# Attention scores and greatest scores as single passes over exact high and low halves, with the shift as a pass of its own

## The chip, the cores and the metric

The kernel runs on one core of a Trainium2 chip. The metric is the device time of one execution in microseconds (us). Three runs of the kernel before gave 1910.36, 1911.48 and 1913.2 us; their median is 1911.48.

The engines of the core that matter here: TensorE (PE in the profile; its weight loads are PEld), VectorE (DVE), ScalarE (ACT), GpSimd (POOL), and Sync (SP), which here only issues DMAs. Each engine takes its instructions in order; they run beside one another and wait for one another by semaphores. TensorE writes its results to eight PSUM banks of 128 x 512 fp32.

## The reference

The model takes 2048 tokens of width 256 and a context of 1601 rows of width 192. A first layer lets the tokens attend to the context once and blends the result in with gates. A second layer, in which most of the time goes, is a transformer block:

```python
def _mha(q_in, kv_in, wq, bq, wk, bk, wv, bv, wo, bo):
    b = q_in.shape[0]
    q = (q_in @ wq.T + bq).reshape(b, -1, HEADS, HD).transpose(0, 2, 1, 3)
    k = (kv_in @ wk.T + bk).reshape(b, -1, HEADS, HD).transpose(0, 2, 1, 3)
    v = (kv_in @ wv.T + bv).reshape(b, -1, HEADS, HD).transpose(0, 2, 1, 3)
    scores = jnp.einsum('bhqd,bhkd->bhqk', q, k) * HD ** (-0.5)
    p = jax.nn.softmax(scores, axis=-1)
    o = jnp.einsum('bhqk,bhkd->bhqd', p, v)
    o = o.transpose(0, 2, 1, 3).reshape(b, -1, WIDTH)
    return o @ wo.T + bo
h = _layernorm(x, ln1_g, ln1_b)
x = x + _mha(h, h, sa_wq, ...)          # self-attention, 2048 keys
h = _layernorm(x, ln2_g, ln2_b)
x = x + _mha(h, context, ca_wq, ...)    # cross-attention, 1601 keys
h = _layernorm(x, ln3_g, ln3_b)
h = jax.nn.gelu(h @ mlp_w1.T + mlp_b1, approximate=False) @ mlp_w2.T + mlp_b2
return x + h
```

There are 16 heads of 16 features (HD). Everything is fp32. The softmax is a true one: each row's greatest score is subtracted.

## The kernel before

**Items and units.** The attention is cut into 32 *items*: one kind (`sa` or `ca`), one block of 512 queries, one group `g` of four heads. An item is cut into *units*, one for each 128 keys: 16 for self-attention, 13 for cross-attention (the last of these has 65 keys). `ITEMS` (L613) lists the items, `groups` (L625) all 464 units. Head `j` of a group has the 32 SBUF partitions from 32 x j on, 16 of which hold its features; so the four heads of a group use four different row groups of TensorE, and four matmuls run abreast.

**A unit.** `scores` (L718) computes keys x queries of one head into a bank, 128 keys by 512 queries, and ScalarE takes the exponential of it into a tile `pt` (L726). The row's greatest score must be subtracted before. It lies in a 17th row: the keys have rows of ones beside their features (`ones_beside`, L560) and the query tile `qa` has the negative greatest score in row 16 (`HD`) of each head, so the same matmul subtracts it. `values` (L731) multiplies the exponentials of the unit before with the values, four heads abreast in four column groups, into one bank, which ScalarE copies to `part` (L751) and GpSimd adds to the item's sum (L752).

**Greatest scores.** They are computed ahead, with the same products in the other orientation: `mx_block` (L664), 128 queries by 512 keys, reduced by VectorE straight from the bank (L680). `lead_unit` (L893) does such a group of four for the first `AHEAD` = 19 units before the attention loop starts; after that, each unit `u` of the loop does the four of unit `u + 19`, so the last 19 units have none. When an item's are complete, `mx_finish` (L701) reduces them, transposes them, sends them through DRAM and copies them into row 16 of `qa`.

**The order.** Compute instructions are kept in the order of the program by `kept`. `ORDER` (L629) is the order of one unit: score, greatest, score, greatest, and so on, then the values of the unit before. `later` (L633) hangs other steps onto the end of a unit: the divisions, the output projection, the layer normalisation of a finished block of queries, the next projection of queries (`q_block`, L639), and `q_spread`. Banks are given out in rotation (`bank`, L550), eight of them, nine to a unit. DMAs are not held to the program's order: they stand in their queue where the framework puts them, and start as soon as what they need is there and the queue has come to them.

**Queries and keys.** A projection gives eight heads on 128 partitions without gaps. `spread` (L592) copies the four heads of one group to their places by four DMAs of 16 partitions. `q_spread` (L657) does so for an item's queries, called four units ahead of the item's first greatest scores, into one of three tiles, plus a DMA that sets row 16 to zero. `k_sa_block` (L1063) does it for a block of 512 keys and half the heads, on the Sync queue, `k_ca_spread` (L1099) for the context's keys on ScalarE's queue.

**Ahead of the loop.** `FIRST` (L1117) is an order written out by hand of the gates of the first layer, the key and value blocks, the first queries and the leading units. The first layer itself, with `mean_context` (L363), comes before that. The MLP follows the attention.

Of the kernel before, what the change touches and what calls it, by code (L numbers as in the profile page):

```python
# [8 lines left out]
F32 = mybir.dt.float32  # L9
AF = mybir.ActivationFunctionType  # L10
# [4 lines left out]
P = 128  # L15
S = 2048
D = 256
# [12 lines left out]
EPS = 1e-5  # L30

# [39 lines left out]
def xattn_kernel(  # L71
# [464 lines left out]
    def load_wo(pool, w, name, queue):  # L536

        t = pool.tile([P, G // 2, D], F32, name=name)
        v = w.rearrange("(pr hf j w) n -> hf j w pr n", hf=2, j=4, w=HP)
        for hf in range(2):  # L540
            for j in range(4):
                r = j * HP + hf * HD
                dma = queue.dma_start(t[r : r + HD, :, :], v[hf, j, :HD])
                if queue is nc.gpsimd:
                    kept(dma)
        return t
# [13 lines left out]
    def ones_beside(queue, k, src, gs=range(G)):  # L560
        for g in gs:
            for j in range(4):
                queue.dma_start(k[j * HP + HD : (j + 1) * HP, g, :], src)

# [8 lines left out]
    nc.gpsimd.memset(hT_sa[:HD, 0, :], 1.0)  # L573
    ones_beside(nc.sync, k_sa, hT_sa[:HD, 0, :])
# [17 lines left out]
    def spread(queue, dst, src, hf):  # L592

        for j in range(4):
            r = (hf * 4 + j) * HD
            queue.dma_start(dst[j * HP : j * HP + HD], src[r : r + HD])
# [3 lines left out]
    shs, qa_bufs = [], []  # L600
    for i in range(2):
        sh = lead.tile([P, HP], F32, name=f"sh{i}")
        nc.gpsimd.memset(sh, 0.0)
        shs.append(sh)
    for i in range(3):
        qa = lead.tile([P, QB], F32, name=f"qa{i}")
        nc.gpsimd.memset(qa, 0.0)
        qa_bufs.append(qa)
    zero = lead.tile([4, QB], F32, name="zero")
    nc.gpsimd.memset(zero, 0.0)  # L610
# [18 lines left out]
    ORDER = "s0 m2 s1 m3 s2 m0 s3 m1 a".split()  # L629
    qas, mxps, oTs, hTs = {}, {}, {}, {"sa": {}, "ca": {}}  # L630
# [5 lines left out]
    def normed_block(pre, qb):  # L636
        return hT_sa[:, :, qb * QB : (qb + 1) * QB] if pre == "sa" else hTs["ca"][qb]

    def q_block(pre, qb):  # L639

        h = normed_block(pre, qb)
# [14 lines left out]

    def q_spread(n):  # L657
# [3 lines left out]
        spread(nc.sync, qas[n], normed_block(pre, qb)[:, g // 2, :], g % 2)  # L661
        nc.sync.dma_start(qas[n].rearrange("(j w) n -> w j n", w=HP)[HD], zero)

    def mx_block(n, i, j):  # L664
# [5 lines left out]
        mx = bank()  # L670
        if i < 4 * full:
            kb, qt = divmod(i, 4)
            mm(
                mx,
                qas[n][r, qt * P : (qt + 1) * P],
                kt[pre][r, g, kb * QB : (kb + 1) * QB],
                start=True,
                stop=True,
            )
            kept(nc.vector.tensor_reduce(mxps[n][:, j, qt, kb : kb + 1], mx, AX.X, ALU.max))  # L680
        else:
            left = L - full * QB
            for qt in range(4):
                mm(
                    mx[:, qt * left : (qt + 1) * left],
                    qas[n][r, qt * P : (qt + 1) * P],
                    kt[pre][r, g, full * QB :],
                    start=True,
                    stop=True,
                    skip_group_check=True,  # L690
                )
            kept(
                nc.vector.tensor_reduce(
                    mxps[n][:, j, :, full],
                    mx[:, : 4 * left].rearrange("p (t k) -> p t k", t=4),
                    AX.X,
                    ALU.max,
                )
            )

    def mx_finish(n):  # L701

        sh = shs[n % 2]
        kept(
            nc.vector.tensor_reduce(  # L705
                sh[:, :16].rearrange("p (j t) -> p j t", j=4), mxps[n], AX.X, ALU.max, negate=True
            )
        )
        shT = lead.tile([P, HP], F32, name="shT", bufs=2)
# [3 lines left out]
        nc.sync.dma_start(  # L713
            qas[n].rearrange("(j w) (t a x) -> w j t a x", w=HP, t=4, x=HP)[HD],
            d.rearrange("(a i j t) x -> i j t a x", a=4, i=2, j=4)[0],
        )

    def scores(u, j):  # L718
# [3 lines left out]
        r = slice(j * HP, (j + 1) * HP)  # L722
        sc = bank()
        mm(sc[:kw], kt[pre][r, g, k0 : k0 + kw], qas[n][r, :], start=True, stop=True)
        pt = work.tile([P, QB], F32, name="pt", bufs=8)
        kept(nc.scalar.activation(pt[:kw], sc[:kw], AF.Exp, scale=HD**-0.5))  # L726
        pts[u, j] = pt
# [98 lines left out]
    def norm_steps(kind, qb, ln, bias):  # L826
# [27 lines left out]
        def turn(c):  # L854

            if c == 0 and kind == "mlp":
                hTs.setdefault(kind, {})[qb] = hT_sa[:, :, qb * QB : (qb + 1) * QB]
            elif c == 0:
                hTs.setdefault(kind, {})[qb] = work.tile([P, 2, QB], F32, name="hT", bufs=2)
            pt = bank()  # L860
            for i in range(4):
# [3 lines left out]
                    hTs[kind][qb][:, c, :], pt, AF.Identity,  # L865
# [19 lines left out]
    def ahead(j):  # L885
        k = taken[j]
        n, i = groups[k]
        mx_block(n, i, j)
        taken[j] += 1
# [3 lines left out]
    def lead_unit():  # L893
        for j in (2, 3, 0, 1):
            ahead(j)
# [22 lines left out]
    nTs, rps, us, cands, mvs, devs, hns = ({} for _ in range(7))  # L918
# [96 lines left out]
    def normed_sa(b):  # L1015
        hns[b] = []
        for i in range(4):
            r = res[:, 4 * b + i, :]
            hn = lead.tile([P, D], F32, name="hn", bufs=5)
# [43 lines left out]
    def k_sa_block(b, pr):  # L1063
        k8 = lead.tile([P, QB], F32, name="k8", bufs=3)
        k_block("sa", sa_wk_sb, hT_sa, pr, b * QB, QB, k8)
        for hf in range(2):
            spread(nc.sync, k_sa[:, 2 * pr + hf, b * QB : (b + 1) * QB], k8, hf)
# [5 lines left out]

    ca = {}
# [212 lines left out]
```

## Time and profile before

| | |
|---|---|
| median of three runs | 1911.48 us |
| span of the profiled execution | 1913.1 us |
| first score of the attention loop, from the span's start | 373.3 us |
| granted TensorE clock, mean over the span | 0.997 |
| reduces of greatest scores, VectorE (L680) | 1792 of 681 ns, 1109.2 us |
| exponentials, ScalarE (L726) | 1856 of 602 ns, 959.7 us |
| sums of values, GpSimd (L752) | 414 of 1270 ns, 525.8 us |
| matmuls of self-attention's scores and of its greatest scores (L98) | 2048 instructions each, 520.4 and 502.6 us |
| the same for cross-attention | 1664 and 2048 instructions, 414.6 and 432.4 us |
| matmuls of values (L98) | 2048 and 1664 instructions, 272.8 and 224.9 us |

The profile is of one execution. A group's line gives the source line, engine, operation, written and read tiles, shapes and number, then busy time, mean ns of one, and the idle time of the engine just before them with what ended most of it. All matmuls go through the helper `mm` and so have line L98; they are told apart by their tiles. The second tile named is the moving operand: `bank<-qa,k_sa` is a score, `bank<-k_sa,qa` a greatest score. One fp32 matmul appears as two MATMUL instructions. Matmuls overlap in the pipeline and across the row groups, so busy time on TensorE says little of its own; the distance from start to start does. The timeline gives start, length, engine, line and operation in order of time, with merged neighbours as "x4".

### The profile page before, as it was taken

The numbers are of one execution on the slowest core, as the hardware profiler recorded it, in microseconds if no ns is written. First come the engines' busy times: TensorE is split into PE (matmuls) and PEld (weight loads), VectorE is DVE, ScalarE is ACT, GpSimd is POOL, SyncE is SP. The second block draws the span as 40 slices with busy tenths as digits, with TensorE's granted clock in tenths as the row PEclk, the third lists the DMA queues.
The fourth block names the chain that finished last, engine by engine and source line by source line (L and its number), as shares of the span: only waits on it lengthen the run. The fifth ranks groups of instructions, "written<-read, shape, count | busy, mean of one in ns | idle before, by whom it ended". The sixth has DMA issues, their size and how long they took to land.

```text
span 1913.1 us, 39182 instructions
## 1 busy us (share of the span) xinstructions
PE 1903.8 (100%) x14774; PEld 852.7 (45%) x14774; DVE 1422.8 (74%) x2544; ACT 1339.3 (70%) x2600; POOL 677.9 (35%) x852
## 2 busy tenths in 40 slices
PE   9999999999999999999999999999999999999999
PEld 4769775433333333433333344333333433433466
DVE  3563677888888788878898888888888878886210
ACT  3332433288887888788788887887888788888621
POOL 1203343034444344444354434344444434343010
PEclk8999999999999999999999999999999999999999
DMA  9200405300000000000000000000000000000000
GB/s 227 72 32 20 51 9 95 61 5 5 5 5 5 4 5 5 5 5 5 5 5 5 5 5 5 5 8 4 27 28 4 6 5 5 5 5 2 1 22 22
DMA packets 32894, 38.27 MB, mean 20 GB/s; under 512 B 12416, under 2 KB 25088, under 8 KB 32320
## 3 DMA queue, kind: packets, MB, share of 16 engines
q1 hardware_dynamic: 30880, 29.98, 7.3%
q0 software_dynamic: 1168, 4.11, 0.8%
q10 hardware_dynamic: 656, 1.67, 0.6%
q8 instruction: 116, 1.90, 0.4%
q14 instruction: 74, 0.61, 0.1%
HBM read 16.27 MB, written 2.62 MB: 10 GB/s over the span
## 4 chain that ended last, share of the span: by engine, by line
PE 97%; DVE 3%; DMA 0%; ACT 0%; SPq 0%; issue 0%; DVEq 0%
PE bank L98 86%; PE half L98 9%; DVE mxp L680 2%; PE bank L101 1%; DMA xy_sb<-in_xT_dram 0%; DVE bn_st L837 0%; PE half L101 0%; DVE nr_v L180 0%; PE half L335 0%; DVE mvb L838 0%; ACT xy_sb L385 0%; ACT L726 0%; SPq L108 0%; ACT xy_sb L267 0%; DVE sh L705 0%
## 5 line engine op out<-in xcount | busy, mean ns | idle before, releaser
L680 DVE TENSOR_REDUCE mxp<-bank 128x1 f32<-128x512 f32 x1792 | 1109.2, 681 | 174.1 <-PE bank L98 167.6
L726 ACT ACTIVATE pt<-bank 128x512 f32<-128x512 f32 (+1 forms) x1856 | 959.7, 602 | 201.5 <-PE bank L98 201.0
L752 POOL TENSOR_TENSOR acc<-acc,part 128x512 f32<-128x512 f32 x414 | 525.8, 1270 | 831.8 <-ACT part L751 831.8
L98 PE MATMUL bank<-qa,k_sa 32*128 32x512 f32 x2048 | 520.4, 615 | 0.4
L98 PE MATMUL bank<-k_sa,qa 32*128 32x512 f32 x2048 | 502.6, 617 | 0.1
L98 PE MATMUL bank<-k_ca,qa 32*128 32x512 f32 (+1 forms) x2048 | 432.4, 531 | 0.0
L98 PE MATMUL bank<-qa,k_ca 32*128 32x512 f32 (+1 forms) x1664 | 414.6, 617 | 0.0
L98 PEld LDWEIGHTS bank<-qa,k_sa 32*128 32x128 f32 x2048 | 216.6, 183 | 226.9 <-DVE mxp L680 203.6
L98 PE MATMUL bank<-pt,v_sa 128*32 128x512 f32 x2048 | 272.8, 605 | 0.0
L751 ACT COPY part<-bank 128x512 f32<-128x512 f32 x414 | 252.7, 610 | 12.9 <-PE bank L98 9.8
L98 PEld LDWEIGHTS bank<-qa,k_ca 32*128 32x128 f32 (+1 forms) x1664 | 166.3, 179 | 179.4 <-DVE mxp L680 143.4
L98 PEld LDWEIGHTS bank<-k_sa,qa 32*128 32x128 f32 x2048 | 196.8, 183 | 69.5 <-ACT pt L726 45.4
L98 PE MATMUL bank<-pt,v_ca 128*32 128x512 f32 (+1 forms) x1664 | 224.9, 605 | 0.0
L98 PEld LDWEIGHTS bank<-k_ca,qa 32*128 32x128 f32 x2048 | 196.4, 184 | 47.3 <-ACT pt L726 32.7
L98 PEld LDWEIGHTS bank<-pt,v_sa 128*32 128x32 f32 x2048 | 40.3, 108 | 192.1 <-ACT pt L726 191.1
L98 PEld LDWEIGHTS bank<-pt,v_ca 128*32 128x32 f32 (+1 forms) x1664 | 34.6, 108 | 150.7 <-ACT pt L726 148.6
L1205 DVE TENSOR_TENSOR o<-bank,res 128x512 f32<-128x512 f32 (+1 forms) x9 | 5.6, 631 | 97.0 <-PE bank L98 97.0
L98 PE MATMUL half<-ctx_w,xy_sb 128*128 128x512 f32 (+5 forms) x256 | 74.0, 529 | 0.4 <-ACT xy_sb L385 0.4
L98 PE MATMUL half<-l_pT,ctx 32*128 32x256 f32 (+1 forms) x1632 | 70.9, 376 | 0.7 <-ACT xy_sb L267 0.5
L98 PEld LDWEIGHTS half<-l_pT,ctx 32*128 32x128 f32 (+1 forms) x1632 | 66.0, 158 | 5.7 <-issue 1.1
L315 ACT ACTIVATE pr_xn<-half,l_nmx 128x801 f32<-128x801 f32 (+1 forms) x32 | 29.4, 925 | 50.4 <-DVE l_nmx L312 50.4
L98 PE MATMUL bank<-hT_sa,k_sa 128*128 128x512 f32 x128 | 55.7, 593 | 0.0
(187 smaller groups left out, 1275.5 us busy)
## 6 DMA issues: line engine op xcount, KB each, us to landing
ctx<-l_pT SPq DMA_DIRECT2D x8, 312.0 KB
ctx<-l_pT SPq DMA_DIRECT2D x8, 288.0 KB
xy_sb<-in_xT_dram SPq DMA_DIRECT2D x4, 512.0 KB
res<-in_x_dram SPq DMA_DIRECT2D x4, 512.0 KB
k_sa<-hT_sa SPq DMA_DIRECT2D x16, 128.0 KB
k_sa<-k SPq DMA_DIRECT2D x64, 32.0 KB
qa<-hT_sa SPq DMA_DIRECT2D x64, 32.0 KB
qa<-hT SPq DMA_DIRECT2D x64, 32.0 KB
```

The source lines that it names most:

```text
L98: kept(nc.tensor.matmul(out_, lhsT, rhs, **kw))
L101: kept(nc.tensor.transpose(out_, in_, ident))
L315: nc.scalar.activation(pr_xn[:, t % 2, k0 : k0 + kw], pieces[i], AF.Exp, bias=nmx, scale=1.0 / 16.0, accum_out=dens[:, t, i : i + 1],)
L680: kept(nc.vector.tensor_reduce(mxps[n][:, j, qt, kb : kb + 1], mx, AX.X, ALU.max))
L726: kept(nc.scalar.activation(pt[:kw], sc[:kw], AF.Exp, scale=HD**-0.5))
L751: kept(nc.scalar.copy(part, av))
L752: kept(nc.gpsimd.tensor_add(accs[n], accs[n], part))
L1205: kept(nc.vector.tensor_add(o[:, some, :], po[:, :n, :], res[:, t0 : t0 + n, :]))
```

## The change

Queries and keys are split into two halves of the mantissa each. The high half is the number with its lowest 12 bits cleared (a bitwise AND on VectorE, `halved`), the low half is what is left (a subtraction on GpSimd, in place). Scores are then computed on operands declared `float32r` in place of fp32, which the change calls single passes (`one_pass`).

A head's 32 rows hold the high half of its 16 features and below it the low half (keys), and twice the high half or twice the low half (queries, two tiles `qh` and `ql`). So a first pass with `qh` gives high x high + low x high, and a second with `ql`, into the same bank, the other two products. For scores a third pass over two rows adds the shift: a tile of ones against a third query tile whose two rows hold the high and low half of the negative greatest score. Greatest scores take two passes, scores three. The rows of ones beside the keys, the zeroing of row 16 and the fixed `sh` tiles go away.

`ORDER` interleaves the passes in fives of four heads; the values of the unit before come after all of them, as they did. `spread` is called twice as often for keys (both halves) and four times as often for queries (both halves, twice each). The halves of a pair of items are made at the even one of them; the odd one finds them made. The shift goes to its tile by two DMAs in place of one.

To make room, the normalised queries of the cross-attention lie in `hT_sa`, the third set of query tiles, the output weights of the cross-attention and the ones tile are put into the loop's pool, the MLP's weights into `v_sa`, and its hidden layer into a new pool.

```diff
+HIGH = -(1 << 12)
...
-    nc.gpsimd.memset(hT_sa[:HD, 0, :], 1.0)
-    ones_beside(nc.sync, k_sa, hT_sa[:HD, 0, :])
...
-    def spread(queue, dst, src, hf):
+    def halved(x, hi):
+        kept(nc.vector.tensor_scalar(hi.bitcast(I32), x.bitcast(I32), HIGH, None, ALU.bitwise_and))
+        kept(nc.gpsimd.tensor_sub(x, x, hi))
+
+    def spread(queue, dst, src, hf, at):
 
         for j in range(4):
             r = (hf * 4 + j) * HD
-            queue.dma_start(dst[j * HP : j * HP + HD], src[r : r + HD])
+            queue.dma_start(dst[j * HP + at : j * HP + at + HD], src[r : r + HD])
...
+    def query_tiles(pool, i):
+        qa_bufs.append([pool.tile([P, QB], F32, name=f"{x}{i}", bufs=1) for x in ("qh", "ql", "shift")])
...
+    def one_pass(out_, lhsT, rhs, **kw):
+        mm(out_, lhsT.bitcast(F32R), rhs.bitcast(F32R), skip_group_check=True, **kw)
...
-    ORDER = "s0 m2 s1 m3 s2 m0 s3 m1 a".split()
+    ORDER = (
+        "s0.0 m2.0 s1.0 m3.0 s0.1 m2.1 s1.1 m3.1 s0.2 s1.2 s2.0 s3.0 "
+        "m0.0 m1.0 s2.1 s3.1 m0.1 m1.1 s2.2 s3.2"
+    ).split()
...
     def q_spread(n):
         pre, qb, g = ITEMS[n]
         qas[n] = qa_bufs[n % 3]
         mxps[n] = lead.tile([P, 4, 4, 4], F32, name="mxp", bufs=3)
-        spread(nc.sync, qas[n], normed_block(pre, qb)[:, g // 2, :], g % 2)
-        nc.sync.dma_start(qas[n].rearrange("(j w) n -> w j n", w=HP)[HD], zero)
+        lo = normed_block(qb)[:, g // 2, :]
+        if g % 2 == 0:
+            his[n // 2] = lead.tile([P, QB], F32, name="qhi", bufs=1)
+            halved(lo, his[n // 2])
+        for dst, src in zip(qas[n], (his[n // 2], lo)):
+            for at in (0, HD):
+                spread(nc.sync, dst, src, g % 2, at)
+    def mx_pass(n, i, j, p):
...
+        q = qas[n][p]
+        if p == 0:
+            mxs[j] = bank()
+        mx = mxs[j]
         if i < 4 * full:
             kb, qt = divmod(i, 4)
-            mm(
+            one_pass(
                 mx,
-                qas[n][r, qt * P : (qt + 1) * P],
+                q[r, qt * P : (qt + 1) * P],
                 kt[pre][r, g, kb * QB : (kb + 1) * QB],
-                start=True,
-                stop=True,
-            )
-            kept(nc.vector.tensor_reduce(mxps[n][:, j, qt, kb : kb + 1], mx, AX.X, ALU.max))
+                start=(p == 0),
+                stop=(p == 1),
+            )
+            if p == 1:
+                kept(nc.vector.tensor_reduce(mxps[n][:, j, qt, kb : kb + 1], mx, AX.X, ALU.max))
...
     def mx_finish(n):
...
+        kept(
+            nc.vector.tensor_scalar(
+                sh[:, :16].bitcast(I32), least.bitcast(I32), HIGH, None, ALU.bitwise_and
+            )
+        )
+        kept(nc.vector.tensor_sub(sh[:, 16:], least, sh[:, :16]))
...
+        for i in range(2):
+            nc.sync.dma_start(
+                qas[n][2].rearrange("(j w) (t a x) -> w j t a x", w=HP, t=4, x=HP)[i],
+                d.rearrange("(a i j t) x -> i j t a x", a=4, i=2, j=4)[i],
+            )
...
+    def score_pass(u, j, p):
...
+        if p == 0:
+            scs[j] = bank()
+        sc = scs[j]
+        rows_of_j = slice(j * HP, (j + 1) * HP if p < 2 else j * HP + 2)
+        keys = kt[pre][rows_of_j, g, k0 : k0 + kw] if p < 2 else ones[rows_of_j, :kw]
+        one_pass(sc[:kw], keys, qas[n][p][rows_of_j, :], start=(p == 0), stop=(p == 2))
+        if p == 2:
+            pt = work.tile([P, QB], F32, name="pt", bufs=8)
+            kept(nc.scalar.activation(pt[:kw], sc[:kw], AF.Exp, scale=HD**-0.5))
+            pts[u, j] = pt
...
     def k_sa_block(b, pr):
-        k8 = lead.tile([P, QB], F32, name="k8", bufs=3)
+        k8 = lead.tile([P, QB], F32, name="k8", bufs=2)
+        hi = lead.tile([P, QB], F32, name="khi", bufs=1)
         k_block("sa", sa_wk_sb, hT_sa, pr, b * QB, QB, k8)
+        halved(k8, hi)
         for hf in range(2):
-            spread(nc.sync, k_sa[:, 2 * pr + hf, b * QB : (b + 1) * QB], k8, hf)
+            for at, half_ in ((0, hi), (HD, k8)):
+                spread(nc.sync, k_sa[:, 2 * pr + hf, b * QB : (b + 1) * QB], half_, hf, at)
...
     def k_ca_spread(pr):
+        halved(ca["k8"][pr], ca["hi"])
         for hf in range(2):
-            spread(nc.scalar, kt["ca"][:, 2 * pr + hf, :], ca["k8"][pr], hf)
+            for at, half_ in ((0, ca["hi"]), (HD, ca["k8"][pr])):
+                spread(nc.scalar, kt["ca"][:, 2 * pr + hf, :], half_, hf, at)
...
     for u in range(NU - AHEAD, NU):
-        for j in range(4):
-            scores(u, j)
+        for p in range(3):
+            for j in range(4):
+                score_pass(u, j, p)
         values(u - 1)
```

## The prediction

> **What bounds the kernel now.** I read the page first (busy times, the chain that ended last, the costliest groups), then the timeline of a few units of attention, the Sync queue's timeline ahead of the attention loop, and the chain in order of time.
>
> ```profile
> PE 1903.8 (100%) x14774; PEld 852.7 (45%) x14774; DVE 1422.8 (74%) x2544; ACT 1339.3 (70%) x2600; POOL 677.9 (35%) x852
> ...
> L680 DVE TENSOR_REDUCE mxp<-bank 128x1 f32<-128x512 f32 x1792 | 1109.2, 681 | 174.1 <-PE bank L98 167.6
> L726 ACT ACTIVATE pt<-bank 128x512 f32<-128x512 f32 (+1 forms) x1856 | 959.7, 602 | 201.5 <-PE bank L98 201.0
> L752 POOL TENSOR_TENSOR acc<-acc,part 128x512 f32<-128x512 f32 x414 | 525.8, 1270 | 831.8 <-ACT part L751 831.8
> ```
>
> TensorE is never without work, and the idle time of VectorE and ScalarE ends with a bank that TensorE fills. One unit (of 464; the first 445 also compute greatest scores) in the timeline, columns start, length, engine:
>
> ```profile
> 999.80 0.69 PE L98 MATMUL bank<-qa,k_sa 32*128 32x512 f32 x1
> ...
> 1000.33 0.59 PE L98 MATMUL bank<-qa,k_sa 32*128 32x512 f32 x1
> ...
> 1000.77 0.59 PE L98 MATMUL bank<-qa,k_sa 32*128 32x512 f32 x1
> ...
> 1001.00 2.48 DVE L680 TENSOR_REDUCE mxp<-bank 128x1 f32<-128x512 f32 x4 [0.45 <-PE bank L98]
> 1001.01 2.06 ACT L726 ACTIVATE pt<-bank 128x512 f32<-128x512 f32 x4 [0.39 <-PE bank L98]
> 1001.19 0.59 PE L98 MATMUL bank<-k_sa,qa 32*128 32x512 f32 x1
> ...
> 1001.73 1.07 PE L98 MATMUL bank<-pt,v_sa 128*32 128x512 f32 x8
> 1002.72 0.69 PE L98 MATMUL bank<-qa,k_sa 32*128 32x512 f32 x1
> ```
>
> Eight fp32 matmuls, two instructions each, run four abreast: four rounds of 0.43 us start to start, the first 0.10 longer (0.53) because its weight load lies open. The last round streams until 1001.63; values start 0.10 later and take 0.99 to the next unit. The unit is 2.93 us. VectorE needs 2.4 of it (0.60 start to start for a reduce), ScalarE about 2.5 (0.49 for each of four exps and a copy). So TensorE cannot bring a unit below about 2.5, and VectorE sits at its limit in units that carry more: in the chain four reduces and one statistic fill a unit.
>
> ```profile
> 69.93 21.95 PE half L98 x400
> ...
> 597.08 2.38 DVE mxp L680 x4
> 599.45 0.35 DVE bn_st L837
> ```
>
> The Sync queue ahead of the loop, and the first score matmul (the tile view of the query tiles gives the loop's start):
>
> ```profile
> 285.45 12.20 SPq L596 DMA_DIRECT2D k_sa<-k  x16
> ...
> 320.49 4.94 SPq L596 DMA_DIRECT2D k_sa<-k  x8
> ...
> 364.82 0.69 SPq L712 DMA_DIRECT2D sh_dram<-shT  x1
> 367.73 0.60 SPq L713 DMA_DIRECT2D qa<-sh_dram  x1
> ...
> 419.26 2.49 SPq L596 DMA_DIRECT2D qa<-hT_sa  x4
> ```
> ```profile
> L98 PE MATMUL bank<-qa,k_sa x2048: 586/587/692, 373.3 to 1479.4; 32*128 32x512 f32 x187
> ```
>
> A copy costs the queue 0.62 to 0.63 us. The queries of an item are copied as soon as their tile is free (419 is the end of item 0, thirteen units before item 3 is needed).
>
> **The change, part by part.** *The price of a pass.* No row shows a single-pass matmul. One fp32 matmul is two instructions with a weight load each; an exact product of two split operands has four partial products, so each instruction should stream its columns twice. The lower bound is half of 0.43, 0.215; the upper is a whole instruction, 0.43. The row nearest to the new pace is mean_context: 32x128 weights, four abreast, 400 matmuls of 256 columns in 21.95 us, a round (a load and a matmul in each row group) every 21.95 / 102 = 0.215 (408 instructions in 102 rounds; some records are missing). So loads and issue can keep that pace, and I take 0.215.
>
> The Trainium skill ("FP8 and Floating Point Precision", TensorE Precision Notes) says that true FP32 takes four passes and that a reduced form truncates to FP22; no run here shows the reduced form, and it gives no time. Its "TensorE: Matmul & The Clock Gate" (Part 3, what overlaps) says that a weight load hides under a running matmul only in another row group, which speaks against five short passes that each reload their own row group. The 0.215 round above and the single open load per unit disagree. By the rule the two further rounds ahead of the first exp would each show a load of 0.10, the unit would be 2.89 instead of 2.69, and the sum some 70 us higher; by the row it is as follows.
>
> *A unit.* Eight matmuls (four rounds of 0.43) become twenty passes (five of 0.215). TensorE alone: 0.10 + 5 x 0.215 + 0.10 + 0.99 = 2.27. But the values' output bank is the one that the unit's first score left (eight allocations back, before and after), so values wait for that exp, and its third pass ends only at 0.10 + 3 x 0.215 = 0.75. The exp starts 0.25 after its stream (today 1000.33 + 0.43 to 1001.01), takes 0.60, and I add 0.09 to the values' start, as today's changeover: 1.69. With 0.99: 2.68, against 2.93. What is late next is ScalarE, with 0.15 of slack, and VectorE with 0.28. Of the 445 units, seven stretches of 13 behind a query block's end carry projection and normalisation and stand at VectorE's limit; for these 91 I take 0.10, the others 0.245: 354 x 0.245 + 91 x 0.10 = **-96 us** (bounds: 445 x 0.43, ScalarE's limit, -191; and the rise if a pass is 0.43, below).
>
> *Waits for queries.* Splitting is new in the order of VectorE and GpSimd: for even items the bitwise AND stands behind the reduces of the fourth unit ahead of the first use, so these copies can't run early any more. The AND of 128x512 is not shown; tensor_scalar rows of 128x256 take 0.40 and 0.61, so 0.4 to 1.2, taken 0.6. From the end of that unit: reduces still run 0.5, AND 0.6, then 16 copies instead of 4: the low half's last copy issues at 1.1 + 15 x 0.63 = 10.6 and lands 1.7 later (sh_dram's round trip and the query copies show 1.5 to 1.7): 12.3. The subtraction (1.27, like the L752 adds) lies under the first eight copies. The second pass wants it at 3 x 2.68 + 0.3 = 8.3. TensorE waits 4.0, with all scores queued behind it. Fifteen items in the loop are even; seven lie in stretches whose units are up to 2.5 longer, where I take 1.5: 8 x 4.0 + 7 x 1.5 = **+42 us** (bounds 0, if the copies run earlier, and 15 x 4.0 = 60). Odd items' halves exist already and their copies run ahead. The shift's extra copy (0.6 per item) has some four units of cover; without it each item would wait 0.6.
>
> *Ahead of the loop.* Eight key blocks of 16 copies instead of 8, and items 0 and 1 with 16 each: 160 copies x 0.63 = 101 us on Sync from about 286.5 (one AND after 285.45), to 387.5. The removed row of ones beside the keys saves 32 copies, of which 16 stood in gaps before and 16 in an idle stretch, so nothing on this path; the zero copies too. Then item 0's shift: 2.9 (364.82 to 367.73), two copies 1.2, landing 1.7: 393.3, against 373.3: **+20 us**. The 19 leading units save 0.43 each, 8 us, under this queue. Bounds: -8 (the 64 copies for the later heads fall behind the shift: 96 x 0.63 ends at 347, before today's), and +40 (the high half's single buffer makes VectorE, with the reduces and value tiles queued behind it, wait for twelve copies of the block before; and the context keys' 32 copies on ScalarE's queue, 0.6 each, 16 more than now).
>
> *Small.* Two more VectorE operations per item at 0.21 (like L705 and L710), 13 us, mostly in slack: **+5** (0 to 13). The moved MLP buffers, the value-weight load and the ones tile cost nothing where the loop covers them; uncovered, the eight weight copies are 5 us. The last 19 units run at ScalarE's four exps already: 0. Sum: -96 + 42 + 20 + 5 = -29 on 1913.1, so 1884; the runs' median is 1.6 lower, and I say **1883 us**.
>
> **Rivals.** *A pass costs an instruction of today, 0.43.* Then TensorE's own unit is 0.10 + 5 x 0.43 + 0.10 + 0.99 = 3.34: 445 x 0.41 = +182, waits 8 x 2 = 16, +20 and +5: 2136. For it: each instruction in the trace streams 512 columns in 0.43. Against it: the four partial products. The unit is 2.04 + 3 passes; the 29 us are gone after 0.065 per unit, so from 0.237 a pass the change loses. Chance 0.14.
>
> *Copies cost more than matmuls gain*: the three upper bounds, 60 + 40 + 13 - 96 = +17: 1930. For it: Sync's 0.63 and the single buffer. Against: the longer units in seven of the stretches. Chance 0.17.
>
> *The copies stay hidden* (the 42 is 0): 1913 - 71 - 2 = 1840. For it: Sync idles nearly all of the loop. Against: the AND's place. Chance 0.16.
>
> **How the numbers follow.** The forecast has 0.53, with its own range 1860 to 1910. Within 0.2% (3.8 us, what the runs can't tell from no change) lie 0.02 of it and 0.02 of the second rival; 0.01 of it and 0.15 of the second are slower, as is the first. Faster 0.50 + 0.16 = 0.66, same 0.04, slower 0.30. The range leaves out the first rival and 0.06 more: 1832 to 1935.
>
> **What would show it.** One MATMUL per pass and rounds of 0.215 (0.43 for the first rival); plain units of 2.68 with values released by the unit's first exp; a gap of TensorE of 4 us at a second pass of mx_pass, released by a DMA into the low-half tile, once per even item; the first score at about 393. It is wrong if plain units stay at 2.9, if those gaps are missing, or if the loop starts as early as now.

## The result and the profile after

The changed kernel takes 1957.7 us (median of four runs, 1953.6 to 1960.07) against 1911.61 us for the kernel before: 1.0234 of it, with a 95% interval of 1.0217 to 1.025. The forecast was 1883 us and faster, so it had the wrong sign. The profiled execution has a span of 1956.8 us at a mean granted clock of 0.954; before it was 1913.1 us at 0.997.

The page of the changed kernel: busy times, the granted clock in 40 slices, the chain of waits by engine, and three of the costliest groups.

```profile
PE 1835.3 (94%) x16630; PEld 938.0 (48%) x16630; DVE 1451.5 (74%) x2634; ACT 1339.3 (68%) x2600; POOL 712.3 (36%) x864
...
PEclk9999996979989999999999999999999999999999
...
PE 72%; DVE 18%; SPq 4%; DMA 3%; issue 1%; POOL 0%; ACTq 0%; ACT 0%; DVEq 0%; POOLq 0%
...
L699 DVE TENSOR_REDUCE mxp<-bank 128x1 f32<-128x512 f32 x1792 | 1111.6, 682 | 148.0 <-PE bank L101 138.9
...
L101 PE MATMUL bank<-k_sa,ql 32*128 32x512 f32 x1024 | 280.5, 424 | 24.8 <-DMA ql<-hT_sa 24.8
...
L101 PE MATMUL bank<-k_ca,ql 32*128 32x512 f32 (+1 forms) x1024 | 240.2, 377 | 19.8 <-DMA ql<-hT_sa 19.5
```

TensorE is no longer always at work. The second passes of the greatest scores, which read the low halves of the queries, wait 24.8 and 19.8 us for DMAs. One more view, TensorE's waits from 425 to 1800 us (us in total, times, longest):

```profile
PE bank L101 <- DMA ql<-hT_sa: 40.9, 17, 3.8
PE bank L101 <- DVE mxp L699: 30.4, 66, 1.5
```

The kernel before has no row in that view.

A plain unit (one without statistics or a projection) in the timeline:

```profile
464.61 0.49 PE L101 MATMUL bank<-qh,k_sa 32*128 32x512 f32 x1
...
464.95 0.39 PE L101 MATMUL bank<-ql,k_sa 32*128 32x512 f32 x1
...
465.18 0.39 PE L101 MATMUL bank<-shift,ones 2*128 2x512 f32 x1
...
465.38 5.00 DVE L699 TENSOR_REDUCE mxp<-bank 128x1 f32<-128x512 f32 x8 [1.63 <-PE bank L101]
...
465.66 2.07 ACT L761 ACTIVATE pt<-bank 128x512 f32<-128x512 f32 x4 [0.27 <-PE bank L101]
...
466.12 0.16 PEld L101 LDWEIGHTS bank<-pt,v_sa 128*32 128x32 f32 x8 [0.38 <-DVE mxp L699]
...
467.12 0.49 PE L101 MATMUL bank<-qh,k_sa 32*128 32x512 f32 x1
```

Every pass is one MATMUL, and a round of four row groups follows the last after 0.23 us (464.95 to 465.18). The first round takes 0.34, its weight load lying open. This unit takes 2.51 us; the next takes 2.80. Over the 445 units the trace gives 2.70 us as the mean of those under 3 us, where it was 2.93.

The experiments below are compared by four times taken from each kernel's one profiled execution: the first score of the attention loop; the first values; the loop, from the first values to the values of the last unit that also computes greatest scores; and the time on record at half of TensorE's clock, in stretches that begin within the loop.

| kernel | median us | ratio to before (95%) | first score | first values | loop | at half clock |
|---|---|---|---|---|---|---|
| before | 1911.61 | 1 | 373.3 | 379.0 | 1373.6 | 0 |
| after | 1957.70 | 1.0234 (1.0217 to 1.0250) | 409.4 | 424.4 | 1373.2 | 119.5 |
| e1_early | 2039.75 | 1.0674 (1.0637 to 1.0711) | 410.8 | 426.4 | 1449.4 | 215 |
| e2_warm | 1937.75 | 1.0130 (1.0115 to 1.0145) | 410.5 | 426.3 | 1349.9 | 10.2 |
| e3_ones | 1954.49 | 1.0204 (1.0158 to 1.0251) | 414.8 | 428.2 | 1371.9 | 116.1 |
| e4_khi2 | 1948.28 | 1.0170 (1.0143 to 1.0198) | 405.9 | 422.3 | 1368.0 | 109.2 |
| f1_lead7 | 1883.19 | 0.9836 (0.9802 to 0.9870) | 410.9 | 426.6 | 1295.4 | 34.1 |
| f2_caq | 1949.81 | 1.0187 (1.0154 to 1.0220) | 409.2 | 422.9 | 1372.8 | 116.1 |
| f3_pool | 1930.06 | 1.0088 (1.0073 to 1.0103) | 390.0 | 407.6 | 1360.8 | 92.2 |
| f4_both | 1863.04 | 0.9734 (0.9719 to 0.9749) | 392.2 | 410.6 | 1293.2 | 27.3 |
| g1_scalar_queue | 1860.05 | 0.9726 (0.9708 to 0.9745) | 392.0 | 402.8 | 1298.5 | 41.0 |
| g2_half_reduce | 1825.46 | 0.9544 (0.9523 to 0.9565) | 409.5 | 425.1 | 1238.7 | 0 |
| h1_sub_pool | 1861.86 | 0.9727 (0.9711 to 0.9743) | 409.5 | 424.2 | 1276.5 | 3.4 |
| h2_best | 1840.38 | 0.9616 (0.9601 to 0.9631) | 394.1 | 404.7 | 1278.2 | 6.8 |

Between before and after, then, the loop starts 45.4 us later, by its first values (36.1 by its first score), and is no shorter, although nearly every unit in it is. The stretch behind the loop changed by 1.3 us.

The first wait of an even item, in the timeline of the changed kernel:

```profile
453.79 5.70 SPq L600 DMA_DIRECT2D ql<-hT_sa  x8
...
456.47 0.49 PE L101 MATMUL bank<-ql,k_sa 32*128 32x512 f32 x1
...
460.39 0.47 PE L101 MATMUL bank<-k_sa,ql 32*128 32x512 f32 x1 [3.43 <-DMA ql<-hT_sa]
...
460.92 0.62 PE L101 MATMUL bank<-k_sa,ql 32*128 32x512 f32 x1
...
462.75 1.93 PE L101 MATMUL bank<-pt,v_sa 128*32 128x512 f32 x8
...
466.13 1.07 PE L101 MATMUL bank<-pt,v_sa 128*32 128x512 f32 x8
```

The low half's eight copies leave Sync from 453.79 to 459.49; TensorE comes to the first pass that reads them at about 457 and stands still for 3.43 us. Then something comes that the forecast has no term for: the same eight value matmuls take 1.93 us at 462.75 and 1.07 us at 466.13. The trace records half the granted clock from 461.1 to 464.5, 3.41 us. All such stretches that begin in the loop are one, two or three times 3.41 us long, 119.5 us together. Each of the fifteen waits of over 1 us for queries (1.08 to 3.79 us) is followed by one, and so are six of the seven gaps of 1.53 us in which TensorE waits for VectorE.

### The profile page after: what moved, and what is told of

It reads as the page before. It is cut to its first block, busy times and chain, and to the rows that moved or that the text cites. A ratio compares the mean times of both kernels' runs of the same rounds, so it can differ in the third digit from the quotient of the medians.

```text
span 1956.8 us, 43902 instructions
## 1 busy us (share of the span) xinstructions
PE 1835.3 (94%) x16630; PEld 938.0 (48%) x16630; DVE 1451.5 (74%) x2634; ACT 1339.3 (68%) x2600; POOL 712.3 (36%) x864
## 3 DMA queue, kind: packets, MB, share of 16 engines
q8 instruction: 131, 2.15, 0.4%
HBM read 16.53 MB, written 2.62 MB: 10 GB/s over the span
## 4 chain that ended last, share of the span: by engine, by line
PE 72%; DVE 18%; SPq 4%; DMA 3%; issue 1%; POOL 0%; ACTq 0%; ACT 0%; DVEq 0%; POOLq 0%
PE bank L101 62%; DVE mxp L699 13%; PE half L101 9%; SPq L600 4%; DMA ql<-hT_sa 2%; PE bank L104 1%; DVE avT L809 1%; DMA k_sa<-khi 1%; DVE sh L736 0%; DVE bn_st L872 0%; DVE oT L822 0%; ACTq L600 0%; DVE rs L811 0%; DMA xy_sb<-in_xT_dram 0%; DVE mvb L873 0%
## 5 line engine op out<-in xcount | busy, mean ns | idle before, releaser
L101 PE MATMUL bank<-shift,ones 2*128 2x512 f32 (+1 forms) x1856 | 400.8, 409 | 9.2 <-POOL ones L1177 9.2
L101 PE MATMUL bank<-k_sa,qh 32*128 32x512 f32 x1024 | 316.1, 494 | 27.5 <-DMA qh<-qhi 11.4
L101 PE MATMUL bank<-k_sa,ql 32*128 32x512 f32 x1024 | 280.5, 424 | 24.8 <-DMA ql<-hT_sa 24.8
L101 PE MATMUL bank<-qh,k_sa 32*128 32x512 f32 x1024 | 286.9, 481 | 0.0
L101 PE MATMUL bank<-k_ca,qh 32*128 32x512 f32 (+1 forms) x1024 | 263.1, 432 | 0.0
L101 PE MATMUL bank<-k_ca,ql 32*128 32x512 f32 (+1 forms) x1024 | 240.2, 377 | 19.8 <-DMA ql<-hT_sa 19.5
L101 PE MATMUL bank<-ql,k_sa 32*128 32x512 f32 x1024 | 250.0, 452 | 0.0
L101 PE MATMUL bank<-qh,k_ca 32*128 32x512 f32 (+1 forms) x832 | 223.0, 472 | 0.0
L101 PEld LDWEIGHTS bank<-shift,ones 2*128 2x128 f32 (+1 forms) x1856 | 195.2, 190 | 17.3 <-POOL ones L1177 9.6
L101 PE MATMUL bank<-ql,k_ca 32*128 32x512 f32 (+1 forms) x832 | 194.9, 431 | 0.0
```

What stands on the lines that cost most here:

```text
L101: kept(nc.tensor.matmul(out_, lhsT, rhs, **kw))
```

## The experiments on the loop

**e2_warm.** Five dummy fp32 matmuls ahead of the second pass of each even item keep TensorE busy while the copies arrive.

```diff
         n, i = groups[k]
+        if n > 1 and n % 2 == 0 and i == 0 and j == 2 and p == 1:
+            busy = bank()
+            for _ in range(5):
+                mm(busy, ident, hT_sa[:, 0, :QB], start=True, stop=True)
         mx_pass(n, i, j, p)
```

> The wait for an even item's low half stays, but five fp32 matmuls of 512 columns (some 4.3 us of work on identity, into a bank that nobody reads) stand ahead of the waiting pass, so that TensorE is busy in the wait. Theory A1 (a part of the loss is the clock that is halved after a gap): the half clock in the loop goes, the 4.2 us units behind the waits fall to about 2.8, and the time falls by 20 to 45 us. Theory B1 (the units behind a wait are long because the pipeline refills): the clock recovers but the time changes by less than 8 us.

One such burst in its timeline:

```profile
651.29 4.56 PE L101 MATMUL bank<-hT_sa,ident 128*128 128x512 f32 x10
```

Time at half clock fell from 119.5 to 10.2 us and the kernel became 20 us faster, though it computes more: theory A1, at the lower edge of its 20 to 45 us. The fifteen bursts cost 15 x 4.56 = 68 us and took the place of 41 us of waiting, 27 more, and the loop is still 23 us shorter. So 109 us at half clock had cost about 50.

**e1_early and f1_lead7.** These issue the split and the copies of an item's queries nine or seven units ahead of its greatest scores instead of four.

```diff
-        later(START[n][0] - AHEAD - 4, lambda n=n: q_spread(n))
+        later(START[n][0] - AHEAD - 7, lambda n=n: q_spread(n))
```

> Queries of an item are split and copied nine units ahead of their first use instead of four. Theory A (the late low-half copies, and the half clock that follows each wait, cost the loop what the passes gained): the fifteen long units of 6 to 8 us and the 4.2 us units behind them fall to 2.6 to 3 (4.4 where an output projection stands), the half clock in the loop (119 us of it in the changed kernel) all but goes, the time falls by 70 to 100 us to 1860 to 1890, below the kernel before. Theory B (VectorE is the loop's bound and the waits only give it time to catch up): the waits go but other units grow, and the time falls by less than 25 us.

Both theories missed; the run says nothing about them. An item's query tiles are those of the third item before it, and where the two items between are of cross-attention, with 13 units each, a lead of nine refills them, in the program's order, one unit before the last scores that read them. Those scores are then computed from other queries, and TensorE waits for the copies: 46.1 us for high halves and 50.5 us for low halves. With a lead of seven no tile is refilled early (by the same count not with eight either, which was not tried).

> Splitting and copying an item's queries starts seven units ahead of their first use instead of four, the earliest at which the tile of the third item before is free in the program's order. Theory A (the late copies and the half clock after them): the waits at the low halves go, the half clock in the loop falls from 119 us to under 20, the loop from 1373 to 1270 to 1295 us, the time to 1855 to 1885, below the kernel before. Theory B (the waits only cover VectorE's backlog): the loop stays above 1350 us.

In f1_lead7 the view of TensorE's waits from 425 to 1800 us has a single row:

```profile
PE bank L101 <- DVE mxp L699: 35.1, 67, 1.8
```

The 40.9 us on copies are gone, half clock falls by 85 us, and the loop by 78 us: 41 are the waits themselves, so the 85 us of half clock had cost 37, or 0.43 us for each (e2_warm gives 0.46). Both are remainders of sums; TensorE's waits for VectorE, 4.7 us longer here than in the changed kernel, are not taken out. This one number makes the change pay: 1883.19 us, 0.9836 of before. That is theory A, though the half clock left, 34.1 us, is above the 20 it allowed, and the loop just past its 1295.

**h1_sub_pool.** What is left in f1_lead7 are ten gaps of TensorE of 1.5 to 1.8 us, eight of them followed by half clock. One, in the timeline of f1_lead7:

```profile
640.09 0.22 DVE L727 TENSOR_REDUCE least<-mxp 128x16 f32<-128x64 f32 x1
...
640.23 1.28 POOL L787 TENSOR_TENSOR acc<-acc,part 128x512 f32<-128x512 f32 x1 [1.63 <-ACT part L786]
...
640.34 1.20 DVE L732 TENSOR_SCALAR sh<-least 128x16 int32<-128x16 int32 x1
...
641.57 0.17 DVE L736 TENSOR_TENSOR sh<-least,sh 128x16 f32<-128x16 f32 x1
...
642.15 2.48 DVE L699 TENSOR_REDUCE mxp<-bank 128x1 f32<-128x512 f32 x4
...
642.89 1.07 PE L101 MATMUL bank<-pt,v_sa 128*32 128x512 f32 x8 [1.78 <-DVE mxp L699]
```

The AND over 128x16 elements takes 1.20 us, where it takes 0.17 in most items, and ends 0.03 us after a sum on GpSimd (640.23 to 641.51) that had started before it. In f1_lead7 three ANDs and seven subtractions are stretched to 1.20 to 1.30 us; each ends 0.02 to 0.04 us after such a sum, and the ten places are those of the ten gaps. All the others take 0.17 to 0.18. The Trainium skill ("SBUF — State Buffer", Who interferes with whom) has this as a rule: VectorE shares one pair of ports with GpSimd; an instruction with two SBUF inputs, or in a mode that uses both ports, and a GpSimd instruction that reads SBUF exclude each other, and the one that starts first keeps the ports to its end. The traces agree: the subtractions have two inputs, and the sums had started 0.005 to 0.02 us before them (0.11 before the ANDs). In five other items the sum had started 0.003 to 0.005 us before; there the subtraction took its 0.17 us, and the sum 1.32 to 1.33 us instead of 1.27 to 1.28. That the ANDs run in such a mode is shown by no run except through their times. The edit puts the subtraction ahead of the sum in GpSimd's own order:

```diff
-        kept(nc.vector.tensor_sub(sh[:, 16:], least, sh[:, :16]))
+        kept(nc.gpsimd.tensor_sub(sh[:, 16:], least, sh[:, :16]))
```

> As f1_lead7 (1883 us), with one edit: the subtraction that makes the shift's low half (128x16) runs on GpSimd instead of VectorE, ahead of the sum of values in GpSimd's order. In f1_lead7 VectorE's AND and subtraction of the shift take 0.17 us each, but in ten of the 32 items one of them takes 1.20 to 1.30 and ends 0.03 us after a GpSimd sum that lies over it; TensorE has ten gaps of 1.5 to 1.8 us in the same places, and eight of them are followed by a stretch at half clock (34 us in all). Theory A (VectorE's small operation is held until GpSimd's sum has ended; reduces behind it are late, TensorE waits, the clock falls): no stretched AND, the ten gaps under 1 us, half clock in the loop under 10 us, loop 1262 to 1282 instead of 1295, time 1850 to 1871. Theory B (statistics make VectorE late in these units anyway): at least six of the ten gaps stay, half clock stays over 20 us, loop 1288 to 1300, time 1876 to 1890.

The same place in the timeline of h1_sub_pool:

```profile
636.35 0.17 DVE L732 TENSOR_SCALAR sh<-least 128x16 int32<-128x16 int32 x1
...
636.60 0.22 POOL L736 TENSOR_TENSOR sh<-least,sh 128x16 f32<-128x16 f32 x1 [2.00 <-DVE sh L732]
...
636.78 1.26 POOL L787 TENSOR_TENSOR acc<-acc,part 128x512 f32<-128x512 f32 x1
636.86 0.21 DVE L738 STREAM_TRANSPOSE shT<-sh 128x32 f32<-128x32 f32 x1 [0.34 <-POOL sh L736]
636.99 1.08 DVE L183 TENSOR_SCALAR nr_v<-mvb 128x4 f32<-128x4 f32 x1
```

GpSimd cannot start the sum before the small operations are done. All 32 ANDs take 0.174 to 0.176 us, VectorE's wait for GpSimd is 0.34, half clock in the loop falls to 3.4 us, and the loop by 18.9: theory A. Three gaps of 1.8 us remain, at 637.1, 976.5 and 1310.4, so "the ten gaps under 1 us" was not met in full. The last row shows the likely reason: the delayed sum now holds a statistics operation, which takes 1.08 us at 637.0, 976.4 and 1310.3 and 0.16 in the other query blocks. The kernel before had three of these too (1.09 us), without a gap of TensorE above 1 us.

**g2_half_reduce.** f1_lead7 with the reduces halved, so the greatest score over half of the keys in blocks of 512 is left out.

```diff
-                kept(nc.vector.tensor_reduce(mxps[n][:, j, qt, kb : kb + 1], mx, AX.X, ALU.max))
+                kept(nc.vector.tensor_reduce(mxps[n][:, j, qt, kb : kb + 1], mx[:, : QB // 2], AX.X, ALU.max))
```

> As f1_lead7, but every greatest-score reduce of a block of 512 keys reads only its first 256 columns: the greatest score over the other half of these keys is left out. This asks what sets the plain unit of 2.70 us. Theory A (VectorE: the bank that the values take is handed back by the unit's first reduce, and the second passes of the greatest scores wait for reduces): a reduce falls from 0.60 to about 0.35 start to start, the values start about 0.25 earlier, plain units at 2.45 to 2.55 (ScalarE's four exps and a copy are then the limit), loop 1200 to 1245 instead of 1295, time 1790 to 1835. Theory B (the unit's first exp hands the bank back, as the prediction had it): plain units stay at 2.65 to 2.70, only units with statistics and projection get shorter, loop 1270 to 1295, time 1860 to 1885.

Neither theory holds whole. Plain units stay (2.66 us, theory B's figure), but the loop falls by 57 us to theory A's 1239. The gain is mostly in the units with statistics, projection and the held operations: units over 3.5 us are 23 with 106 us, against 47 with 202 in f1_lead7, those from 3 to 3.5 us 20 with 65, against 50 with 157. The plain units, 0.03 us shorter each, give some 12 of the 57 us. VectorE bounds the long units, and not the plain ones. A part of that goes by way of the clock: the 34.1 us at half clock are gone too, by estimate 15 us at 0.43 each. ScalarE in the plain ones, in the timeline of g2_half_reduce:

```profile
1062.57 2.07 ACT L761 ACTIVATE pt<-bank 128x512 f32<-128x512 f32 x4 [0.25 <-PE bank L101]
1064.49 0.62 ACT L786 COPY part<-bank 128x512 f32<-128x512 f32 x1
1065.10 2.07 ACT L761 ACTIVATE pt<-bank 128x512 f32<-128x512 f32 x4
1067.02 0.62 ACT L786 COPY part<-bank 128x512 f32<-128x512 f32 x1
1067.89 2.07 ACT L761 ACTIVATE pt<-bank 128x512 f32<-128x512 f32 x4 [0.24 <-PE bank L101]
```

ScalarE's four exps and one copy take 2.53 us without a wait (1064.49 to 1067.02), and every second unit adds 0.24 us in which ScalarE waits for a bank. TensorE's loads in that unit wait in turn for that copy (1065.16, 0.30 us). So VectorE's halved work buys next to nothing there: TensorE and ScalarE hand banks to each other at 2.53 and 2.80 us by turns. That this hand-over alone sets the 2.66 was not tried.

## The experiments ahead of the loop

Sync's queue of the changed kernel, and the waits of all engines from 280 to 430 us:

```profile
384.82 1.22 SPq L600 DMA_DIRECT2D ql<-hT_sa  x2
395.87 2.79 SPq L600 DMA_DIRECT2D k_sa<-khi  x4
398.76 2.43 SPq L600 DMA_DIRECT2D k_sa<-k  x4
401.23 3.27 SPq L600 DMA_DIRECT2D k_sa<-khi  x4
404.55 2.61 SPq L600 DMA_DIRECT2D k_sa<-k  x4
407.26 0.53 SPq L740 DMA_DIRECT2D sh_dram<-shT  x1
```
```profile
ACT k L1074 <- DMA k_ca<-k_hi: 27.6, 1, 27.6
DVE khi L593 <- DMA k_sa<-khi: 25.7, 4, 12.9
...
POOL ones L1177 <- DMA k_ca<-k: 15.5, 1, 15.5
...
PE bank L101 <- POOL ones L1177: 9.2, 1, 9.2
```

Sync issues 160 copies between 283.7 and 407.2, the number in the forecast, in 96 us. But it stands idle for 28 more, 9.8 of them at 386, while ScalarE waits 27.6 us behind the context keys' copies on its own queue and VectorE 25.7 behind the single buffer of high halves. The tile of ones lies where the context keys were staged, so its memset waits for the last of those copies; the first shift pass waits 9.20 us for it. TensorE itself, which has no gap above 1 us between 283 us and the first values in the kernel before, has six there now, of 2.12 to 11.42 us, 39.1 together. It is also at half clock for 58.8 us of that time, before for none; what this costs ahead of the loop was not tried by itself. Six runs try the queues and buffers.

**e3_ones**: the ones tile moves to a place that is free early.

```diff
+        ca["ones"] = kv_ca.tile([P, P], F32, name="ones", bufs=1)
+        kept(nc.gpsimd.memset(ca["ones"], 1.0))
...
-    ones = work.tile([P, P], F32, name="ones", bufs=1)
-    nc.gpsimd.memset(ones, 1.0)
+    ones = ca["ones"]
```

> The ones tile of the shift pass lies in the context keys' pool, filled early, instead of in the loop's pool, whose space the context keys' staging still holds. Theory A (the loop's first shift pass waits 9.2 us for that memset): the first values start 5 to 9 us earlier, 5 because item 0's shift itself lands only at about 414 in the changed kernel; the time falls by 5 to 9 us. Theory B (something else is as late): less than 3 us.

The 9.20 us wait is gone and the first values come no earlier (428.2): TensorE waits instead for the shift itself (2.15 us), a query projection (2.62) and the first exps (1.16). The shift left Sync at 411.3 here, 4.0 us later than in the changed kernel, and the first values follow it after the same 17 us. Theory B.

**e4_khi2**: every second self-attention key block puts its high half in a second place.

```diff
-        hi = lead.tile([P, QB], F32, name="khi", bufs=1)
+        hi = lead.tile([P, QB], F32, name="khi", bufs=1) if (b, pr) not in ((0, 1), (1, 1), (3, 0)) else ca["hi"][:, 2 * QB : 3 * QB]
```

> The high halves of the key blocks alternate between two buffers instead of one. Theory A (VectorE's waits for the single buffer, 25.7 us between 280 and 430, hold up the leading units): the first values start 8 to 20 us earlier. Theory B (Sync's 160 copies of 0.63 us set the start whatever VectorE does): the first values move by less than 5 us, and Sync is busy without gaps until the shift of item 0.

The first values come 2 us earlier, nearer to theory B: a second buffer alone doesn't shorten a queue that is busy 96 of 123 us. Sync still isn't busy without gaps, as theory B had it: its 160 copies take 98 of 120 us.

**f2_caq**: e3_ones, and the context keys' copies go from ScalarE's queue to GpSimd's, where they are also held to the program's order.

```diff
-                spread(nc.scalar, kt["ca"][:, 2 * pr + hf, :], half_, hf, at)
+                spread(nc.gpsimd, kt["ca"][:, 2 * pr + hf, :], half_, hf, at)
```

> The context keys' 32 copies are issued on GpSimd's queue instead of ScalarE's, and the ones tile lies in the context keys' pool. Theory A (copies that wait on ScalarE's queue hold up the evictions of the leading stage, and their staging the ones tile): the two gaps of TensorE of 9 us ahead of the loop go, the first values start 10 to 25 us earlier. Theory B (Sync's copies set the start): less than 6 us.

1.5 us: theory B's figure, but not its reason. Item 0's shift left Sync at 396.4, 10.9 us earlier than in the changed kernel, and the loop did not follow. The first exp now waits 9.91 us, until 419.3, for the context keys' copies on GpSimd's queue.

**f3_pool**: f2_caq and e4_khi2, and half of the self-attention key copies leave Sync for GpSimd's queue, which takes 0.50 us for a copy (47.6 us for 96).

```diff
-                spread(nc.sync, k_sa[:, 2 * pr + hf, b * QB : (b + 1) * QB], half_, hf, at)
+                spread(nc.gpsimd if pr else nc.sync, k_sa[:, 2 * pr + hf, b * QB : (b + 1) * QB], half_, hf, at)
```

> As the run before, and the 64 key copies of the later heads also on GpSimd's queue, with two buffers for the high halves: Sync issues 96 copies ahead of item 0's shift instead of 160. Theory A (Sync's queue sets the start): the first values come at 379 to 400 us instead of 424, the time falls by 25 to 45 us. Theory B (the order of VectorE, ScalarE and GpSimd sets it): they come after 410.

The first score comes at 390.0 and the first values at 407.6, 17 us earlier, between the figures of the two theories. With the key copies shared out the start moves, so their queue is a part of the bound. The run joins three edits, and what the first two give together was not tried. It isn't the whole bound either: TensorE still waits 9.92 us at 396.0 for the first exps.

**f4_both**: f3_pool with the lead of seven units.

> The seven units' lead and the queues of the run before together. If both theories A hold and the parts add up: 1820 to 1860 us, 3 to 5% below the kernel before. If the loop is bound by VectorE or the start by another engine: above 1900.

The two gains nearly add: 94.7 us, against 74.5 and 27.6 singly (loop 1293.2, first values 410.6); 1863.04 us is just above the range. ScalarE's first table load shows what is late next, in f4_both and in g1_scalar_queue:

```profile
407.03 1.28 ACT L763 ACT_TABLE_LOAD   x1 [14.59 <-DMA k_ca<-k]
```
```profile
399.21 1.28 ACT L763 ACT_TABLE_LOAD   x1 [7.18 <-DMA k_ca<-k]
```

**g1_scalar_queue**: f4_both with the 16 copies of one key block on ScalarE's queue, held to the program's order there.

```diff
-spread(nc.gpsimd if pr else nc.sync, k_sa[...], half_, hf, at)
+spread(nc.scalar if (b, pr) == (2, 1) else nc.gpsimd if pr else nc.sync, k_sa[...], half_, hf, at)
```

> As f4_both, with the 16 copies of one self-attention key block (rows 1024 to 1535, second half of the heads) on ScalarE's queue instead of GpSimd's. In f4_both the first exp waits 14.59 us, until 407.0, for the last copies of the context keys, which stand on GpSimd's queue behind these 16 (7.9 us of issue). Theory A (that queue still sets the loop's start): the last context copy is issued 6 to 8 us earlier, first values at 402 to 405 instead of 410.6, loop unchanged at 1293, and the time 5 to 9 us below f4_both: 1854 to 1859. Theory B (something else is as late: the shift, the query projection behind ScalarE's 16 copies, at 0.6 each until about 391, or the slow clock): first values within 2 us of 410.6 or later, time 1861 to 1870.

The first exps start 7.8 us earlier and the first values come at 402.8, as theory A says. The time does not follow (1860.05; the intervals of the two overlap): in the profiled execution the loop is 5 us longer, with 14 us more at half clock. So far as one profile of each shows, a gain ahead of the loop of this size can drown as long as held operations throw the clock.

**h2_best**: g1_scalar_queue with h1_sub_pool's edit.

> As g1_scalar_queue (1860 us), with the same edit as h1_sub_pool: the shift's low half is subtracted on GpSimd. Theory A: loop 1265 to 1285 instead of 1298.5, half clock in the loop under 10 us instead of 41, first values unchanged at about 403, time 1827 to 1847. Theory B: within 5 us of g1_scalar_queue.

1840.38 us, 0.9616 of before: the fastest of the kernels that compute all of the reference. Half clock in the loop is 6.8 us: theory A in all its figures.

## Why the prediction was wrong

Term by term, on the profiled executions:

| term | forecast | measured | from |
|---|---|---|---|
| units, with VectorE's small operations | -96 + 5 | -78 | loop of before 1373.6, of f1_lead7 1295.4 |
| waits for queries | +42 | +41 | waits of after, 40.9 |
| half clock behind those waits | none | +37 | 1373.2 - 1295.4 - 40.9 |
| ahead of the loop | +20 | +45 | first values 379.0 and 424.4 (first scores, as forecast: +36) |
| behind the loop | 0 | -1 | |
| sum | -29 | +44 | spans 1913.1 and 1956.8 |

**What failed: the waits as the prediction put them, "8 x 4.0 + 7 x 1.5 = +42 us".** Their length was right to 1 us in the sum; singly the fifteen are 1.08 to 3.79 us long, not 4.0 and 1.5. Their price was not right: a gap of TensorE was taken to cost its own length, and each of the fifteen is followed by 3.41 to 10.24 us at half clock, which nearly doubles it (+37 us that the sum has no term for). That the clock could fall was to be seen before, too: the granted clock was 0.997, with 10.2 us on record at half clock, all in the first 31 us of the span. A change that opens gaps in an engine that had none should have been priced by those rows. The Trainium skill ("TensorE: Matmul & The Clock Gate", Part 1) gives the same window, 3.4 us, and asks for a whole idle window before the clock falls; the traces agree with the length and not with the threshold, since eight of f1_lead7's ten gaps of 1.5 to 1.8 us were followed by half clock. None of the three signs that the forecast named for being wrong came true; it failed by what it left out.

**The second failure: "393.3, against 373.3: +20 us".** The count was right (160 copies, at 0.60 rather than 0.63 us), the gaps were not: 28 us of Sync's idle time were in the upper bound only, as the single buffer and ScalarE's queue. The first score came at 409.4, +36.1, still inside the bound of +40. From there to the first values the kernel before takes 5.7 us and the changed one 15.0, with the wait of 9.20 us for the ones tile, which the forecast had at nothing where the loop covers it. How the 45.4 us divide between the queue, the gaps of TensorE and the half clock stays open: moving copies off Sync and ScalarE and doubling the buffer took 17 of them away together (f3_pool).

**The price of a pass, 0.215, was right** (0.23 in the rounds shown), and with it the fall of the first rival, at 0.43. The plain unit of 2.68 came out at 2.70, but by another way than the prediction's "values wait for that exp": in the unit shown values start at 466.12, the unit's first exp ends at about 466.26, and the load's bracket names VectorE's reduce. Over the whole span the loads for self-attention's values waited for the exp before, and for the reduce after:

```profile
L98 PEld LDWEIGHTS bank<-pt,v_sa 128*32 128x32 f32 x2048 | 40.3, 108 | 192.1 <-ACT pt L726 191.1
```
```profile
L101 PEld LDWEIGHTS bank<-pt,v_sa 128*32 128x32 f32 x2048 | 41.0, 110 | 115.9 <-DVE mxp L699 115.4 <-issue 0.4
```

**"Small: +5"** was too little. An operation of 0.17 us cost 1.2 to 1.3 us where it met GpSimd's sum. h1_sub_pool puts what this did to the loop at 18.9 us in f1_lead7, gaps and clock together. Without it the loop is 97 us shorter than before, close to the forecast's -91.

**The rivals.** Nearest came the second, copies that cost more than the matmuls gain. Its sum of three upper bounds, 1930, had the right sign and was 28 us too low; the clock's 37 us are not in it. The third, hidden copies at 1840, is what h2_best reaches, by other edits.

## What to carry to other kernels

When TensorE is never idle, a change that puts gaps of 1 to 4 us into it must be priced with the half clock that can follow: here 0.43 to 0.46 us for each us on record, nearly as much again as the gaps. Moving the issue of a prefetch by three units turned 2.3% slower into 1.6% faster, so when a change with a good mechanism loses, look first at how early its data is asked for. A queue's count of copies sets a prologue's length only if nothing holds the copies back: follow each buffer they read from, and what is laid over the space they leave.

## What the runs showed that was not expected

- In the changed kernel's loop 21 stretches at half clock begin, and TensorE has 22 gaps of 1.08 to 3.79 us there; 21 of the gaps are followed, 1.3 to 4.2 us after their beginning, by such a stretch. The kernel before has no gap above 1 us in its loop and no such stretch.
- The length of a gap alone does not decide it. Over the eleven traces with such gaps (e1_early left out), all 69 gaps behind copies, 1.03 to 4.09 us long, are followed by half clock, and 46 of the 72 behind VectorE, 1.48 to 1.84 us long. In e4_khi2 one stretch follows a gap of 0.82 us.
- A 128x16 operation on VectorE took 0.17 us, or 1.18 to 1.30 us in thirteen of the 64 in the changed kernel, each of which ends 0.03 us after a GpSimd sum of 128x512 that had started before it.
- A pass over two rows (shift and ones) takes the same time on TensorE as one over 32 rows, 0.39 us in the unit shown.
